# Segment sums, scan and step order in the Mamba mixer of a perceiver block

## The chip, the cores and the metric

The kernel runs on one core of a Trainium2 chip. The metric is device time in microseconds (us), the median of several runs. All arithmetic is float32. A core has five engines with a queue of their own each: TensorE (PE in the profile; its weight loads are PEld), VectorE (DVE), ScalarE (ACT), GpSimd (POOL) and SyncE (SP, which issues the DMAs here). An engine executes its instructions strictly in the order in which they were put down; engines wait for each other by semaphores.

## The reference

A block of three layers with residuals: cross attention of 8 x 64 queries on 8 x 1601 keys (32 heads of 128), a Mamba-2 mixer, and a routed low-rank layer. The change lies in the mixer. Cut to what matters:

```python
proj = einsum('bld,pd->blp', hidden_states, in_proj_w)
gate, hbc, dt = proj[..., :I], proj[..., I:I+CONV_DIM], proj[..., -H:]
conv = conv_bias + sum(pad[:, k:k+L, :] * conv_weight[:, k] for k in range(4))
xBC = silu(conv)                      # x: 64 heads x 64, B and C: 8 groups x 128
dt_p = softplus(dt + dt_bias); dA = exp(dt_p * A); dtx = dt_p * x
state = state * dA_t + dtx_t * B_t    # per head, step by step in time
y_t = einsum('bhpn,bhn->bhp', state, C_t)
y = y + x * D
yn = y * rsqrt(mean(y*y over a group of 512) + eps) * norm_weight * silu(gate)
out = einsum('bli,di->bld', yn, out_proj_w)
```

Here B x L is 8 x 64 tokens of width 512; there are 64 heads in 8 groups.

## The kernel before

**Attention** (the first 2290 us or so) is not touched by the change, and the built program's order there is the same but for line numbers. Then the **mixer** goes through 8 groups of 8 heads; the 512 tokens are four tiles of 128, and each tile holds two sequences (b = 0, 1) of 64 tokens. The recurrence is not run step by step: since a sequence has only 64 tokens, y is a 64 x 64 matrix product per head and sequence, whose matrix is C·B times the decay between two time steps. Per group:

- `steps` (GpSimd, L1154): four `av`, one for each tile, from the decay exponents; four buffers.
- `decay` (TensorE L1170, ScalarE L1175): the segment sums `seg` of two tiles at a time, as 64 x 64 matmuls into two banks of tag `seg`, and their exponentials `dec`. It is called twice, for tiles 0, 1 and for tiles 2, 3. Tag `seg` has two buffers, so the second call's matmuls wait until the first call's two exponentials have read the banks.
- `project` (TensorE L1184): ten input projections of 128 channels by 512 tokens. Numbers 0 to 3 are gates, 4 to 7 are x, 8 and 9 are B and C. For 4 to 9 VectorE makes the convolution's four taps out of the bank (`acc`, L1195 for the first tap and L1201 for the three others), ScalarE the silu (`xs` L1209, `bc` L1207); for x, ScalarE also writes `y` = D·x (L1213), VectorE turns `xs` by 32 x 32 blocks (`xt`, L1216), and SyncE sends it through DRAM (`x_d`) and back as `dx`, which GpSimd multiplies by dt (L1294).
- `project_gates` (TensorE L1246): in groups 1 to 7 the gate projections, as a Strassen-like scheme of seven products in two halves, `first` (four products) and `second` (three more into banks a, b, c). Between them ScalarE copies bank a to `p` (L1261) and VectorE reads d, b and c (`u` L1263, `p` L1264, `sg` L1265); `second` writes into these banks again.
- `mix` (L1284 to L1294): the product C·B of a tile (`pg` on TensorE, in a `seg` bank), masked (`gm`, VectorE) and multiplied by `dec` to `m` (VectorE L1291; two buffers).
- `scan` (TensorE L1307, VectorE L1313): 16 matmuls of 64 x 64 for one tile into the banks y0 and y1 (one buffer each), and two additions to `y`.
- `gate` and `squares`: the squares of y (`sq`, ScalarE L1319), their sums over channels (GpSimd L1320 and L1322, result `s`), and y times the gate (VectorE L1329).
- `norm` (TensorE L1335 `pss`, ScalarE L1338 and L1339 `rs`): the sum over channels and its inverse root.
- `project_out` (TensorE L1348 `mo`, VectorE L1352): a tile of the output projection, added to x. Four tiles a group, in one bank.

ScalarE has two function tables in turn: Silu, and Ln with Exp. Each change is a table load: the one placed ahead of `decay` has L121, the one back is put down with the first silu (L1271 or L1207).

The loop over groups is pipelined by one: while group g is projected, group g - 1 (`old`) is mixed, scanned and gated. Which step of `old` stands behind which projection is written out by hand in the loop (L1435 to L1455); there `issue_after` tells the recording layer to put an instruction down no earlier than another, and within such bounds a planner orders each engine's queue by its own estimate of times. So an engine's order can differ from the text. The last group's own steps stand between its gate projections (L1488 to L1510, `own`).

Of the kernel before, what the change touches and what calls it, by code (L numbers as in the profile page):

```python
# [9 lines left out]
F32 = mybir.dt.float32  # L10
# [5 lines left out]
P = 128  # L16
B, S, D = 8, 64, 512
# [24 lines left out]
H2, PD, N2, G2, KC = 64, 64, 128, 8, 4  # L42
I2 = H2 * PD
HPG = H2 // G2
HH = HPG // 2
GC = I2 // G2 // P
# [72 lines left out]
def load_ln_exp(nc):  # L119

    return nc.scalar.preload_act_table_set("natural_log_exp_and_others")  # L121
# [875 lines left out]
def mixer_and_routed(ctx, tc, c, x, done, w_in, w_out, w_ra, b_w, out):  # L997
# [7 lines left out]
    nc = tc.nc  # L1005

    grpp = ctx.enter_context(tc.tile_pool(name="mx_grp", bufs=2))
# [8 lines left out]
    def bank(tag, shape, name, bufs=1):  # L1016
        return (ps4 if tag in ("pj", "y1") else ps).tile(shape, F32, tag=tag, name=name, bufs=bufs)
# [9 lines left out]
    for g in range(G2):  # L1027
        G = Group()
# [3 lines left out]
    def load_in(G):  # L1032
        g = G.g
        G.w = wst.tile([P, DC, 10, P], F32, tag="w_in", name=f"w_in_{g}")
        at = 0
        for lo, n in (
            (g * GC * P, GC), (I2 + g * GC * P, GC), (2 * I2 + g * N2, 1), (2 * I2 + G2 * N2 + g * N2, 1)
        ):
            nc.sync.dma_start(
                out=G.w[:, :, at : at + n, :],  # L1040
                in_=w_in[:, lo : lo + n * P].rearrange("(dc p) (n o) -> p dc n o", p=P, o=P),
            )
            at += n

    def load_out(G):

        g = G.g
        G.wo = wst.tile([P, GC, D], F32, tag="w_out", name=f"w_out_{g}")
        nc.sync.dma_start(
            out=G.wo, in_=w_out[g * GC * P : (g + 1) * GC * P, :].rearrange("(n p) o -> p n o", p=P)  # L1050
        )
# [18 lines left out]
    for tt in range(NTT):  # L1070
# [5 lines left out]
        for dc in range(DC):  # L1076
            nc.tensor.matmul(
                pdt[:, tt, :], lhsT=xnT[:, dc, tok], rhs=c.wdt[:, dc, :],
                start=dc == 0, stop=dc == DC - 1,
# [49 lines left out]
    for r in range(0, P, S):  # L1129
        nc.tensor.matmul(  # L1130
            psw[r : r + S], lhsT=c.ident[:, S - r : 2 * S - r], rhs=a.rearrange("p t h -> p (t h)"),
            start=True, stop=True,
# [12 lines left out]
    def heads(G):  # L1145
        return slice(G.g * HPG, (G.g + 1) * HPG)

    def steps(G, tt):


        if tt == 0:
            G.av, G.dec = [], grpp.tile([P, NTT, HPG, S], F32, tag="dec", name="dec")
        av = wk.tile([P, 2, HH, S], F32, tag="av", name="av", bufs=4)
        nc.gpsimd.tensor_tensor(  # L1154
            av,
            ah[:, :, tt, G.g, :].unsqueeze(3).to_broadcast([P, 2, HH, S]),
            c.upto1.unsqueeze(1).unsqueeze(1).to_broadcast([P, 2, HH, S]),
            ALU.mult,
        )
        G.av.append(av)  # L1160

    def decay(G, tts):


        segs = [bank("seg", [P, 2, HH, S], f"seg{half}", 2) for half in range(2)]
        for i, tt in enumerate(tts):
            for b in range(2):
                for half in range(2):
                    rows = slice(half * S, (half + 1) * S)
                    nc.tensor.matmul(  # L1170
                        segs[half][b * S : (b + 1) * S, i], lhsT=c.past[rows, rows],
                        rhs=G.av[tt][rows, b], start=True, stop=True,
                    )
        for half in range(2):
            last = nc.scalar.activation(  # L1175
                G.dec[:, tts[0] : tts[0] + 2, half * HH : (half + 1) * HH], segs[half], AF.Exp
            )
        return last.ins
# [100 lines left out]
    def mix(G, tt):  # L1279

        tok = slice(tt * P, (tt + 1) * P)

        pg = bank("seg", [P, P], "pg", 2)
        nc.tensor.matmul(pg, lhsT=G.bc[:, 0, tok], rhs=G.bc[:, 1, tok], start=True, stop=True)  # L1284
        gm = grpp.tile([P, S], F32, tag="gm", name="gm", bufs=2)
        for r in range(0, P, S):
            nc.vector.tensor_tensor(
                gm[r : r + S], pg[r : r + S, r : r + S], c.upto1[r : r + S], ALU.mult
            )
        m = grpp.tile([P, HPG, S], F32, tag="m", name="m")  # L1290
        nc.vector.tensor_tensor(  # L1291
            m, G.dec[:, tt], gm.unsqueeze(1).to_broadcast([P, HPG, S]), ALU.mult
        )
        nc.gpsimd.tensor_tensor(  # L1294
            G.dx[tt], G.dx[tt], dt[:, tt, heads(G)].unsqueeze(2).to_broadcast([P, HPG, PD]), ALU.mult
        )
        G.m = getattr(G, "m", {})
        G.m[tt] = m

    def scan(G, tt):  # L1300

        py = [bank(f"y{b}", [P, GC, S], f"py{b}") for b in range(2)]
        for h in range(HPG):
            r0 = (h % 2) * PD
            for b in range(2):
                at = slice(b * S, (b + 1) * S)
                nc.tensor.matmul(  # L1307
                    py[b][r0 : r0 + PD, h // 2, :], lhsT=G.dx[tt][at, h, :], rhs=G.m[tt][at, h, :],
                    start=True, stop=True,
                )  # L1310
        for b in range(2):
            y = G.y[:, :, tt * P + b * S : tt * P + (b + 1) * S]
            nc.vector.tensor_tensor(y, y, py[b], ALU.add)  # L1313

    def squares(G, tt):
# [50 lines left out]
    def load_routed():  # L1366
        nc.sync.dma_start(out=w, in_=w_ra.rearrange("(dc p) o -> p dc o", p=P))
        nc.sync.dma_start(out=bw, in_=b_w)
# [52 lines left out]
    for tt in (0, 2):  # L1421
        last = decay(g0, (tt, tt + 1))
    for g in range(G2):
        G, old = groups[g], groups[g - 1] if g else None
        new = groups[g + 1] if g + 1 < G2 else None
        load_out(G)
        if new:
            load_in(new)
            for tt in range(NTT):
                steps(new, tt)  # L1430
        elif old:
            load_routed()
        silus = []
        with tc.issue_after(last):


            ns = (8, 9, 4, 5, 6, 7) if new else (4, 5, 6, 7, 8, 9)
            if not old:


                ns = (8, 9, 4, 0, 5, 1, 6, 2, 7, 3)
            for n, behind in zip((None,) + ns, (
                ((mix, 0),),
                ((mix, 1),),
                ((scan, 0),),
                ((mix, 2), (scan, 1)),
                ((gate, 0), (mix, 3), (scan, 2)),
                ((gate, 1), (scan, 3)),
                ((gate, 2), (gate, 3)),
            ) if old else ((),) * (len(ns) + 1)):  # L1450
                if n is not None:
                    done, silu = project(G, n)
                    silus.append(silu)
                if old:
                    with tc.issue_after(done if n is not None else done_out):  # L1455
                        for what, tt in behind:
                            what(old, tt)
            load_x(G)
        if not old:
            token_sums()  # L1460
            sums_in(new, 0)
            sums_in(new, 2)
        with tc.issue_after(silus[-1]):
            table = load_ln_exp(nc).ins
        if new:
            with tc.issue_after(table):
                decay(new, (0, 1))
                last = decay(new, (2, 3))
        if old:
            with tc.issue_after(table):  # L1470
                last = norm(old, range(NTT))

        if not old:
            with tc.issue_after(last):
                weigh_out(G)
            done_out = done
            continue

        def own(*what):

            if not new:
                for step, tt in what:
                    step(G, tt)

        done_out = None
        for k in range(2):  # L1488
            first, second = project_gates(G, 2 * k)
            if k:  # L1490
                own((scan, 3), (squares, 3))
            with tc.issue_after(done_out) if k else nullcontext():
                done_out = first()
            if not k:
                own((mix, 0), (mix, 1))
            with tc.issue_after(done_out):
                done_out = project_out(old, 2 * k)
            if not k:
                own((scan, 0), (squares, 0), (mix, 2))
            with tc.issue_after(done_out), tc.issue_after(last):  # L1500
                done_out, last_gate = second()
            if not k:
                own((scan, 1), (squares, 1), (mix, 3))
            with tc.issue_after(done_out):
                done_out = project_out(old, 2 * k + 1)
            if not k:
                own((scan, 2), (squares, 2))
            if new:
                sums_in(new, 2 * k)
        with tc.issue_after(last_gate):  # L1510
            weigh_out(G)
        last = last_gate

    G = groups[-1]
# [80 lines left out]
```

## Time and profile before

| | |
|---|---|
| median of 3 runs | 2762.47 us (2760.94 to 2763.59) |
| span of the profiled execution | 2760.8 us |
| TensorE busy in it | 2734.8 us (99%) |
| VectorE, ScalarE, GpSimd busy | 63%, 28%, 29% |
| TensorE clock granted | 0.9 or more in every slice |
| start of the first projection of group 0 | 2293.96 us |

Busy time of engines by stage, with the second `mo` tile as the mark between groups 2 to 6 (us of the span):

| stage | length | TensorE | VectorE | ScalarE | GpSimd |
|---|---|---|---|---|---|
| 2293.0 to 2341.0 (group 0) | 48.0 | 47.1 | 30.2 | 18.9 | 12.1 |
| 2341.0 to 2376.0 | 35.0 | 33.8 | 28.9 | 15.6 | 15.0 |
| 2376.0 to 2432.0 | 56.0 | 54.7 | 35.5 | 20.2 | 19.8 |
| 2432.0 to 2487.8 | 55.8 | 54.5 | 35.6 | 19.8 | 19.9 |
| 2487.8 to 2543.7 | 55.9 | 54.6 | 35.6 | 19.9 | 20.0 |
| 2543.7 to 2599.6 | 55.9 | 54.6 | 35.6 | 19.9 | 20.0 |
| 2599.6 to 2654.9 | 55.3 | 54.6 | 35.0 | 19.9 | 15.4 |
| 2654.9 to 2701.4 | 46.5 | 46.4 | 32.4 | 14.2 | 15.1 |
| 2701.4 to 2760.8 (own steps of group 7, routed layer) | 59.4 | 53.5 | 33.6 | 18.9 | 9.7 |

A share of busy time says nothing about who sets the end; that is read from the chain of waits. A line of it has a start, a duration, and an engine with the tile and the line. A line of a timeline has start, busy time, engine, line, operation, output and input tiles, shapes, and in brackets the idle time just before it with what ended it. A matmul in float32 is two records, so x16 are eight matmuls.

### The profile page before, as it was taken

The page shows a single profiled execution, that of the slowest core. Times are in us where ns is not written, and L with a number is a line of the kernel's source. Part 1 is how long each engine was busy: PE and PEld are TensorE (multiplying, and loading weights), DVE is VectorE, ACT ScalarE, POOL GpSimd, SP SyncE. Part 2 cuts the span into 40 slices and gives each one's busy share as a digit, 9 for nine tenths or more (in the row PEclk, how much of TensorE's full clock was granted, in tenths as well). Part 3 has the DMA queues.
Part 4 walks back from the last instruction along what each step waited for, and adds up shares of the span by engine and source line. Part 5 has one row for each costly group of instructions (what it writes and reads, how often), then busy time and mean ns, then how long its engine had stood idle before and what let it go on. Part 6 is the DMA issues. An engine that isn't in the chain of part 4 may idle for free.

```text
span 2760.8 us, 38909 instructions
## 1 busy us (share of the span) xinstructions
PE 2734.8 (99%) x14962; PEld 2003.4 (73%) x14962; DVE 1751.8 (63%) x3151; ACT 772.4 (28%) x1374; POOL 811.5 (29%) x810
## 2 busy tenths in 40 slices
PE   9999999999999999999999999999999999999999
PEld 7677787777777777778777777877777654555555
DVE  5666676576666666766666676667666416765676
ACT  3322223222222222222222222223222103333333
POOL 4423323222222233222322222223322212334321
PEclk9999999999999999999999999999999999999999
DMA  4821322131123212221322132122211462333421
GB/s 164 280 90 47 88 66 61 48 104 43 51 54 89 57 39 85 78 56 40 87 71 55 46 97 55 42 77 66 64 49 52 131 213 66 93 95 100 132 64 35
DMA packets 349715, 222.85 MB, mean 81 GB/s; under 512 B 223932, under 2 KB 309050, under 8 KB 348506
## 3 DMA queue, kind: packets, MB, share of 16 engines
q1 hardware_dynamic: 349530, 220.36, 28.3%
q8 instruction: 119, 1.95, 0.3%
q14 instruction: 66, 0.54, 0.1%
HBM read 189.26 MB, written 31.05 MB: 80 GB/s over the span
## 4 chain that ended last, share of the span: by engine, by line
PE 88%; DVE 8%; DMA 2%; ACT 2%; issue 1%; POOL 1%; SPq 0%; DVEq 0%; ACTq 0%; POOLq 0%
PE pav L623 13%; PE psc L553 13%; PE pv_a L472 6%; PE pv_b L472 6%; PE pk_b L412 6%; PE pv_c L472 6%; PE pk_c L412 6%; PE pk_a L412 6%; PE mo L1348 3%; PE pv_d L472 3%; PE pk_d L412 3%; DVE acc L1201 3%; PE psn L441 2%; PE pj L1184 2%; PE pj_ab L1246 1%; PE pvl L495 1%
## 5 line engine op out<-in xcount | busy, mean ns | idle before, releaser
L558 DVE SCALAR_TENSOR_TENSOR attn<-psc,rk,mask_sb 128x256 f32<-128x256 f32 (+1 forms) x832 | 364.3, 476 | 201.3 <-PE psc L553 199.4
L607 POOL TENSOR_TENSOR sm<-attn 128x512 f32<-128x512 f32 x64 | 81.9, 1280 | 1201.5 <-ACT attn L605 1201.5
L623 PE MATMUL pav<-attn,v 128*128 128x256 f32 (+1 forms) x1664 | 380.3, 379 | 0.0
L553 PE MATMUL psc<-q,kT 128*128 128x256 f32 x1536 | 367.1, 380 | 0.0
L610 POOL TENSOR_TENSOR sm<-sm,attn 128x512 f32<-128x512 f32 x256 | 339.8, 1327 | 29.4 <-DVE attn L601 10.2
L553 PEld LDWEIGHTS psc<-q,kT 128*128 128x128 f32 x1536 | 287.6, 190 | 76.3 <-issue 28.6
L623 PEld LDWEIGHTS pav<-attn,v 128*128 128x128 f32 (+1 forms) x1664 | 311.5, 190 | 42.3 <-issue 1.0
L601 DVE TENSOR_TENSOR attn<-attn,nb 128x1024 f32<-128x1024 f32 x192 | 224.8, 1215 | 48.0 <-ACT nb L598 47.7
L605 ACT ACTIVATE attn<-attn 128x1024 f32<-128x1024 f32 x192 | 203.1, 1058 | 79.8 <-DVE attn L601 77.1
L472 PEld LDWEIGHTS pv_a<-wv,cx 128*128 128x128 f32 x1536 | 193.9, 191 | 28.9 <-issue 22.1
L569 DVE TENSOR_TENSOR mx<-mx,attn 128x512 f32<-128x512 f32 x256 | 211.1, 825 | 2.0
L472 PE MATMUL pv_a<-wv,cx 128*128 128x128 f32 x1536 | 206.8, 277 | 0.0
L412 PE MATMUL pk_a<-cx,wk 128*128 128x417 f32 (+1 forms) x512 | 193.3, 500 | 0.8 <-ACT qrs L115 0.8
L1184 PE MATMUL pj<-mx_xnT,w_in 128*128 128x512 f32 x416 | 190.4, 601 | 0.0
L423 ACT ACTIVATE ksq<-kT 128x834 f32<-128x834 f32 (+1 forms) x128 | 109.2, 871 | 144.7 <-DVE kT L404 144.7
L1184 PEld LDWEIGHTS pj<-mx_xnT,w_in 128*128 128x128 f32 x416 | 74.9, 190 | 78.9 <-issue 75.7
L412 PEld LDWEIGHTS pk_a<-cx,wk 128*128 128x128 f32 x512 | 97.2, 190 | 46.1 <-issue 20.8
L1348 PE MATMUL mo<-w_out,y 128*128 128x512 f32 x256 | 115.8, 594 | 0.0
L598 ACT COPY nb<-nbs 128x256 f32<-128x256 f32 x64 | 24.1, 376 | 301.5 <-DMA nbs<-max_d 289.0
L402 ACT COPY kT<-pk_a 128x384 f32<-128x384 f32 x64 | 31.6, 493 | 267.6 <-PE pk_a L412 267.5
L1201 DVE SCALAR_TENSOR_TENSOR acc<-pj,small_consts,acc 128x504 f32<-128x504 f32 x144 | 104.3, 724 | 1.4
L670 POOL TENSOR_TENSOR o<-o,f 128x512 f32<-128x512 f32 x31 | 39.5, 1274 | 221.4 <-DMA f<-sums_d 184.4
(247 smaller groups left out, 4391.8 us busy)
## 6 DMA issues: line engine op xcount, KB each, us to landing
wk<-in_wk SPq DMA_DIRECT2D x32, 512.0 KB
wv<-in_wv SPq DMA_DIRECT2D x32, 512.0 KB
w_in<-in_w_in SPq DMA_DIRECT2D x16, 1024.0 KB
wvs<-wv_s_d SPq DMA_DIRECT2D x28, 512.0 KB
wks<-wk_s_d SPq DMA_DIRECT2D x28, 512.0 KB
cx<-in_ctxT SPq DMA_DIRECT2D x16, 834.0 KB
cx<-in_ctxT SPq DMA_DIRECT2D x16, 768.0 KB
wq<-in_wq SPq DMA_DIRECT2D x16, 512.0 KB
```

Source lines behind the costliest of these rows:

```text
L412: nc.tensor.matmul(ps[:, :w], lhsT=u.wk[l][:, dc, :], rhs=u.cx.r[ch][r][:, dc, :], start=start and dc == 0, stop=dc == 1, skip_group_check ...
L472: nc.tensor.matmul(ps[:, i * HD : (i + 1) * HD], lhsT=u.cx.r[ch][r][:, dc, i * P : (i + 1) * P], rhs=u.wv[l][:, dc, :], start=start and i ...
L553: nc.tensor.matmul(ps[:rows, t - t2, :], lhsT=lhsT, rhs=qh, start=True, stop=True)
L558: nc.vector.scalar_tensor_tensor(out=s.at[:rows, t, :].rearrange("p (h q) -> p h q", h=GQ), in0=ps[:rows, t - t2, :].rearrange("p (h q) -> ...
L569: nc.vector.tensor_tensor(s.mx2, s.mx2, s.at[:, t2 : t2 + 2, :], ALU.max)
L601: nc.vector.tensor_tensor(at[:, k : k + 4, :], at[:, k : k + 4, :], nb.unsqueeze(1).to_broadcast([P, 4, 256]), ALU.add,)
L605: nc.scalar.activation(at[:, k : k + 4, :], at[:, k : k + 4, :], AF.Exp)
L610: nc.gpsimd.tensor_tensor(sm2, sm2, at[:, i : i + 2, :], ALU.add)
L623: nc.tensor.matmul(s.av[:, 0, :], lhsT=u.v[:rows, t, hh, :], rhs=s.at[:rows, t, :], start=t == 0, stop=t == NKT - 1,)
L1184: done = nc.tensor.matmul(pj, lhsT=G.w[:, dc, n, :], rhs=xnT[:, dc, :], start=dc == 0, stop=dc == DC - 1).ins
L1201: nc.vector.scalar_tensor_tensor(out=accb[:, :, k:], in0=pjb[:, :, : S - k], scalar=c.cw[:, ct, KC - 1 - k : KC - k], in1=accb[:, :, k:], ...
L1348: last = nc.tensor.matmul(po, lhsT=G.y[:, n, tt * P : (tt + 1) * P], rhs=G.wo[:, n, :], start=n == 0, stop=n == GC - 1,)
```

## The change

- `decay` puts the segment sums of tiles 2 and 3 into the banks y0 and y1 of the scan instead of the two `seg` banks, so that the second call's matmuls need not wait for the first call's exponentials.
- `m` has four buffers instead of two.
- `scan` takes two tiles: 32 matmuls into y0 and y1, and two additions of 128 x 512 instead of four of 128 x 256. It is called for pair 0 (tiles 0, 1) and pair 1 (tiles 2, 3).
- The hand-written order of the old group's steps is another: scan of pair 0 stands behind projection 4 (with the third `mix` one projection earlier), gate 0 behind 5, gate 1 and scan of pair 1 behind 6. The last group's own steps are placed anew in the same way.
- The core's scratch for DMAs that GpSimd would issue is 1024 bytes instead of the default.

```diff
     def decay(G, tts):
-        segs = [bank("seg", [P, 2, HH, S], f"seg{half}", 2) for half in range(2)]
+        segs = [
+            bank(f"y{half}", [P, 2, HH, S], f"seg{half}") if tts[0] else
+            bank("seg", [P, 2, HH, S], f"seg{half}", 2) for half in range(2)
+        ]
...
-        m = grpp.tile([P, HPG, S], F32, tag="m", name="m")
+        m = grpp.tile([P, HPG, S], F32, tag="m", name="m", bufs=4)
...
-    def scan(G, tt):
-        py = [bank(f"y{b}", [P, GC, S], f"py{b}") for b in range(2)]
-        for h in range(HPG):
-            r0 = (h % 2) * PD
-            for b in range(2):
-                at = slice(b * S, (b + 1) * S)
-                nc.tensor.matmul(
-                    py[b][r0 : r0 + PD, h // 2, :], lhsT=G.dx[tt][at, h, :], rhs=G.m[tt][at, h, :],
-                    start=True, stop=True,
-                )
+    def scan(G, pair):
+        py = [bank(f"y{b}", [P, 2, GC, S], f"py{b}") for b in range(2)]
+        for i in range(2):
+            tt = 2 * pair + i
+            for h in range(HPG):
+                r0 = (h % 2) * PD
+                for b in range(2):
+                    at = slice(b * S, (b + 1) * S)
+                    nc.tensor.matmul(
+                        py[b][r0 : r0 + PD, i, h // 2, :], lhsT=G.dx[tt][at, h, :], rhs=G.m[tt][at, h, :],
+                        start=True, stop=True,
+                    )
         for b in range(2):
-            y = G.y[:, :, tt * P + b * S : tt * P + (b + 1) * S]
+            y = G.y.rearrange("p n (t b s) -> p b t n s", b=2, s=S)[:, b, 2 * pair : 2 * pair + 2]
             nc.vector.tensor_tensor(y, y, py[b], ALU.add)
...
                 ((mix, 0),),
                 ((mix, 1),),
-                ((scan, 0),),
-                ((mix, 2), (scan, 1)),
-                ((gate, 0), (mix, 3), (scan, 2)),
-                ((gate, 1), (scan, 3)),
+                ((mix, 2),),
+                ((scan, 0), (mix, 3)),
+                ((gate, 0),),
+                ((gate, 1), (scan, 1)),
                 ((gate, 2), (gate, 3)),
...
             if k:
-                own((scan, 3), (squares, 3))
+                own((scan, 1), (squares, 2), (squares, 3))
...
             if not k:
-                own((scan, 0), (squares, 0), (mix, 2))
+                own((mix, 2))
...
             if not k:
-                own((scan, 1), (squares, 1), (mix, 3))
+                own((scan, 0), (squares, 0), (squares, 1), (mix, 3))
...
-            if not k:
-                own((scan, 2), (squares, 2))
...
-    nc = bacc.Bacc("TRN2", target_bir_lowering=False, num_devices=1)
+    nc = bacc.Bacc("TRN2", target_bir_lowering=False, num_devices=1, dynamic_dma_scratch_size=1024)
```

In the built program, the new order of the engines in groups 2 to 6 around these steps is: TensorE has the scan of pair 0 between projections 4 and 5, that of pair 1 between 6 and 7, all 16 segment-sum matmuls of the next group in one burst behind projection 7, then the first half of the gate products, the first two matmuls of the first `mo` tile, the four `pss`, the other two matmuls of that tile, and the second half. ScalarE has, from projection 7 on: `xs`, the table load, `y`, four `dec`, the Ln of `rs`, `p`, the Exp of `rs`, the table load back. Before, `p` stood ahead of that `xs`, and TensorE had the second burst of segment sums behind the first `mo` tile and `pss` within the second half of the gate products. GpSimd now has the first `av` of the next-but-one group between the square sums of tile 3.

## The prediction

> **What bounds the kernel now.** I read the page's chain of waits first, then the chain of one mixer group in order of time, then each engine's timeline in that group. Durations are microseconds; L numbers are lines of the kernel before. The page says TensorE:
>
> ```profile
> PE 88%; DVE 8%; DMA 2%; ACT 2%; issue 1%; POOL 1%; SPq 0%; DVEq 0%; ACTq 0%; POOLq 0%
> ```
>
> That is the whole kernel, and most of it is attention, which the change leaves as it is. The change acts after about 2293 us, in eight groups. The chain through the group that I cost (start, duration, what):
>
> ```profile
> 2448.53 3.45 PE pj L1184 x8
> 2451.98 0.03 issue
> 2452.01 0.81 DVE acc L1195
> ...
> 2478.62 0.72 DVE acc L1201
> 2479.35 0.02 issue
> 2479.37 0.63 ACT xs L1209
> 2480.02 1.28 ACT L121
> 2481.32 0.72 ACT y L1213
> 2482.04 0.49 ACT dec L1175
> 2482.53 0.04 issue
> 2482.57 1.58 PE seg L1170 x16
> ...
> 2487.83 3.43 PE mo L1348 x8
> ```
>
> So in the first half of a group the end is set by VectorE, not by TensorE: from the first convolution of projection 8 (2452.01) to the last one of projection 7 (ends 2479.34) VectorE has no gap to speak of, 27.33 us; then ScalarE does xs, the table load, y and the first dec; only then TensorE goes on. From the mo at 2487.83 to the next group's projection 8 TensorE is back to back. The second burst of segment sums is where TensorE waits (start, busy, idle before in brackets):
>
> ```profile
> 2477.68 3.60 PE L1348 MATMUL mo<-w_out,y 128*128 128x512 f32 x8
> 2482.57 1.58 PE L1170 MATMUL seg<-av,past 64*64 64x256 f32 x16 [1.30 <-ACT dec L1175]
> 2484.08 1.13 PE L1246 MATMUL pj_ab<-mx_xnT,w_in 128*128 128x256 f32 x4
> ```
>
> **What the change removes on TensorE.** The second burst goes into the scan's banks, directly behind the first. From 2481.11 (2477.68 plus 3.43 for the mo) to 2484.08 it cost 2.97; as eight more matmuls of one burst it costs about what the first burst did, 1.02 (2473.10 to 2474.12): 1.95 saved. Four scan bursts become two. A scan burst issues for 0.63 (2455.55 to 2456.18), and the projection behind it takes 3.54 instead of the undisturbed 3.43, the one before it 3.52: 0.2 a burst, 0.4 a group. [...]
>
> If TensorE set the end here, a group would lose 2.35. It doesn't, so I follow the chain.
>
> **What takes the wait's place.** In the built program's new order ScalarE has, in groups 1 to 6: xs, table, y, four dec in a row, the Ln of rs (L1338), and only then p (L1261), which before stood ahead of xs. The second half of the gate products may not overwrite bank a until p has read it. So the wait that went from the segment sums comes back at the products, behind four dec and not one. Rows of ScalarE:
>
> ```profile
> 2477.01 0.37 ACT L1261 COPY p<-pj_ab 128x256 f32<-128x256 f32 x1 [1.31 <-PE pj_ab L1246]
> ...
> 2481.94 1.06 ACT L1175 ACTIVATE dec<-seg 128x512 f32<-128x512 f32 x2
> 2484.19 1.08 ACT L1175 ACTIVATE dec<-seg 128x512 f32<-128x512 f32 x2 [1.18 <-PE seg L1170]
> 2486.03 0.26 ACT L1338 ACTIVATE rs<-pss,eps 128x4 f32<-128x4 f32 x1 [0.76 <-PE pss L1335]
> ```
>
> Counted from the start of the first dec: dec starts follow each other by 0.48 (1.06 less one dec's 0.58), so the Ln starts at 1.92, p at 2.10, p ends at 2.47; TensorE is released 0.04 later (as at 2482.53), at 2.51. Three products of 0.86 follow, plus 0.1 to 0.2 after a stop, and bank c also waits until VectorE has done u, p, the x update (which now stands between them) and sg (0.44 + 0.34 + 0.67 + 0.42 after p: 4.36, against 4.25 to 4.4 from TensorE). So the second mo starts 5.2 to 5.35 after the first dec. Before it was 2487.67 - 2481.94 = 5.73. This tail gives 0.45. TensorE itself would be ready for the products at about 2482.7, p ends at about 2483.8: 1.1 of the saved time goes into the new wait. Behind p on ScalarE stand the Exp of rs, the table load and the gates' silu; the second half's mo waits for none of them longer than this.
>
> **The VectorE stretch.** Same work, other order; I add up start-to-start steps taken from the rows at 2452 to 2479. A step is 0.72 for a first tap (0.84 if its second tap comes directly behind), 0.65 and 0.63 for the others between other work, 0.76 directly behind each other, gm 0.13 and 0.26, m 0.60, xt 0.63, gate 0.60. The merged add (128x512) is in no row: at least twice the shorter part of a 128x256 add (0.33 step, 0.41 long), so 0.60 to 0.66; I take m's step, 0.60, as its nearest row (0.68 long, same width). New order: projections 8 and 9 with gm and m of tiles 1 and 2: 2 x 3.76, to 2459.53. Projection 4 and two adds: 0.84 + 0.76 + 0.65 + 0.60 + 0.63 + 0.60, to 2463.61. gm, xt (waits 0.04 for xs), gm, m: to 2465.27. Projections 5 and 6 with gates 0, 1, xt and the second pair's adds: 8.3, to 2473.57. Projection 7 with gates 2, 3 and xt: 0.71 + 0.60 + 0.63 + 0.64 + 0.60 + 0.76 + 0.72, to 2478.2. That is 1.1 less than 2479.34, half of it from fewer adds and less waiting, half from this:
>
> ```profile
> 2476.23 1.02 DVE L1329 TENSOR_TENSOR y<-y,sg 128x512 f32<-128x512 f32 x1
> 2477.82 0.88 DVE L1329 TENSOR_TENSOR y<-y,sg 128x512 f32<-128x512 f32 x1
> ```
>
> A gate otherwise takes 0.69 (2459.40), and in group 6, where no av runs on GpSimd, 0.68 at both places. Here GpSimd's two av run from 2475.66 to 2478.15: 0.33 + 0.19, some 0.55 of the stretch. In the new order av come free at once after the burst (about 2474.9), and GpSimd has the square sum of tile 3 and an av beside gate 3 (2476.2), and that of tile 2 beside gate 2 (2474.3). I take 0.55 again; bounds 0 and 1.1. [...]
>
> Stretch shorter by 0.55, tail by 0.45: **1.0 a group in groups 2 to 5**, 4.0.
>
> **The other groups.** Group 6 has no av before either, so only waiting and adds are saved, 0.35 + 0.45: 0.8. Group 1: TensorE now stops at pg, whose bank the first dec frees (2335.82 plus about 0.35, since one more projection matmul of 0.86 comes after the first merged burst, whose second half waits for the av anyway), and projection 8 is done at about 2339.9 as before; its stretch, added the same way, ends at 2367.5 to 2368 against 2367.80, and the x update ahead of p on VectorE eats the tail: 0. Group 7 has no dec. There both tiles' squares now come after one pair's adds: adds end about 2697.7, two squares (0.63), two sums on GpSimd of 1.0 and 0.9 each (2699.07 to 2701.02 for one tile now), so the last pss is at 2701.6 to 2702.3, not 2701.08, and mo follows: 0.9 to 1.5 lost; its own four scans as two bursts give back 0.4. Net 0.8 lost. m with four buffers lets m of tiles 1 and 2 be made before the first scan; the stretch has the same count of them, so nothing. The smaller DMA scratch: no row of the trace shows a transfer from GpSimd's queue (q1 is the only data queue), so 0.
>
> Sum: 4.0 + 0.8 + 0 - 0.8 = 4.0 off the profiled execution: span 2760.8, 1.7 below the median of 2762.47. So 2756.8 for its span, 2758.5 for the median; I say **2758**. A measurement of this kernel can tell about 0.2% from no change, 5.5 us: below 2756.9 is faster, above 2768.0 slower. Bounds: merged add 0.60 to 0.66 (0.25 a group), GpSimd 0 to 1.1 (0.55 either way), tail 0.35 to 0.55: 1.0 is 0.2 to 1.65 a group, times five, group 1 and 7 +-0.7: 2754 to 2763 for this case.
>
> **Rivals.** (1) TensorE is the bound and what it saves comes off: 2.35 x 6 = 14, 2748. For it: the page's 99% busy and 88% of the chain. Against: the chain above, 30.5 of a group's 55.9 us (2452.0 to 2482.5) through VectorE and ScalarE, and p behind the dec. Something of it would show if p's wait were hidden: 1.1 a group more, 2752. Chance 0.17 for 2754 or less.
> (2) Nothing left: av slow both gates fully, adds slow, 2761 to 2767. For it: order puts av between the sums. 0.18.
> (3) Slower: two squares now stand together on ScalarE ahead of xs, and four VectorE instructions per group (gate 0, xt, gate 2, xt) are queued right behind them with as little as 0.03 to spare. Each that waits for one square costs 0.63; all four are 2.5 a group, 1.5 net, times five, plus 0.8: 2770. It decides from about 2 us of such waits a group. Against: my times have each of them just ready. 0.08.
> (4) The burst isn't one: its second half must wait for the second pair's adds. They end at about 2473.0, the half is due at 2473.9; and if late, up to 5 us are covered by the stretch. It changes no time, and is within the forecast.
> Forecast 0.57. Of it some 0.25 lie below 2756.9. Faster: 0.17 + 0.25 = 0.42; slower 0.08 and 0.02 from (2): 0.10; within: 0.48. Range 2752 to 2764, leaving about one in ten on each side.
>
> **What would show it.** Right: one burst of 32 seg records a group, no wait there; a wait of about 1 us at pj_ab's second products, released by p; last tap of projection 7 at 26.6 to 27 us after the first; groups 55.87 apart now 54.9; group 7 a little longer. Wrong: if TensorE has no wait at p, (1); if VectorE's stretch is 27.3 or more with waits for ScalarE's squares, (3) or (2).

## The result, and the profile after

The changed kernel is slower: 2781.33 us median of 4 runs (2778.49 to 2785.69), against 2762.19 (2760.94 to 2763.59) for the kernel before on the same chip. The ratio is 1.0071, 95% interval 1.0057 to 1.0086; I had said 2758. The profiled execution has a span of 2776.7 us, 15.9 more than before. Attention ended 2.2 us earlier in it; in the profiles of all the kernels here, which share it, its end varies from 2291.8 to 2296.5. The mixer's groups 0 and 1 lost 5.2 together, group 2 3.3, groups 3 to 5 2.15 each, group 6 2.25, group 7 1.6, and what follows gained 0.7. Of the kernels below, busy3, segs_only and segs_back_busy2 had one execution each that was disturbed and took two to four times as long; the ratios leave it out, it shifts a median by 0.3 us at most, and in segs_back_busy2 it is the profiled one, so that there is no profile to compare.

I take the same group as in the prediction (line numbers from `scan` on are a few higher now). The chain of waits of the changed kernel, in order of time (start, duration, what):

```profile
2458.31 0.81 DVE acc L1198
...
2485.11 0.74 DVE acc L1204
2485.87 0.63 ACT xs L1212
2486.52 1.28 ACT L121
2487.82 0.72 ACT y L1216
2488.54 0.49 ACT dec L1178
2489.03 0.14 issue
2489.16 1.02 PE pss L1340 x8
2490.19 3.16 PE mo L1353 x4
...
2496.30 3.43 PE mo L1353 x8
```

Up to the first dec the chain is the old one: VectorE from 2458.31 to 2485.85 (27.54 us; 27.33 before), then ScalarE. The burst of segment sums that waited for this dec is gone from the chain, and `pss` stands in its place. From the start of the first dec (2488.44) to the second mo (2496.13) it is 7.69 us; before it was 5.73. TensorE's timeline of the changed kernel there:

```profile
2478.62 2.32 PE L1173 MATMUL seg<-av,past 64*64 64x256 f32 x32
...
2484.43 1.88 PE L1353 MATMUL mo<-w_out,y 128*128 128x512 f32 x4
2489.16 1.02 PE L1340 MATMUL pss<-ones,s 128*128 128x1 f32 x8 [2.86 <-ACT dec L1178]
2490.05 3.30 PE L1353 MATMUL mo<-w_out,y 128*128 128x512 f32 x4
2493.15 1.42 PE L1249 MATMUL pj_ab<-mx_xnT,w_in 128*128 128x256 f32 x4
```

The one burst is there (32 records), and no wait in it. But `pss` is a tile of tag `seg`, whose two banks hold the sums of tiles 0 and 1 until the first dec has read one of them. It stands after two of the first mo tile's matmuls, so TensorE stops for 2.86 us in the middle of that tile, and everything behind stops with it. All six groups with a next group do this: `pss` waits 16.0 us for `dec` in all.

The second thing to see is the length of the two mo matmuls behind the stop: 3.30 us, where the tile's other two, ahead of it, took 1.88. The windows of the same stretch (start and end, length, busy time with counts of PE, PEld, DVE, ACT and POOL, then the granted TensorE clock, DMA share and GB/s):

```profile
2484.43:2486.30 1.87, 1.87 (x5) 0.57 (x3) 1.37 (x3) 0.43 (x1) 1.87 (x3) 1.00 0.45 71
2486.30:2489.10 2.80, 0.01 (x1) 0.00 (x0) 0.71 (x1) 2.77 (x5) 1.45 (x2) 1.00 0.28 44
2489.10:2490.00 0.90, 0.84 (x8) 0.87 (x8) 0.00 (x0) 0.90 (x3) 0.00 (x0) 1.00 0.75 117
2490.00:2493.10 3.10, 3.10 (x6) 1.32 (x6) 0.84 (x2) 2.28 (x5) 0.00 (x0) 0.59 0.37 103
2493.10:2494.40 1.30, 1.30 (x5) 1.05 (x4) 0.94 (x2) 0.00 (x0) 0.00 (x0) 0.68 1.00 293
```

After the stop the granted clock falls. The 0.59 and 0.68 are means of windows that lie partly in the drop; cut at its edges, it is half the clock, from 2490.53 to 2493.94:

```profile
2489.90:2490.50 0.60, 0.60 (x4) 0.42 (x4) 0.00 (x0) 0.60 (x4) 0.00 (x0) 1.00 0.51 81
2490.55:2493.90 3.35, 3.35 (x6) 1.66 (x5) 1.28 (x3) 1.73 (x4) 0.00 (x0) 0.50 0.48 164
2493.95:2496.10 2.15, 2.15 (x11) 1.89 (x10) 0.59 (x2) 0.38 (x1) 0.58 (x1) 1.00 0.81 225
```

By the rows it costs 1.44 us on the two mo matmuls (3.16 in the chain, less 2 x 0.86) and 0.40 on the two products behind (2493.15 to 2494.41, 1.26 and not 0.86): 1.84 of the group's 2.15. That is a little too much, since two mo matmuls directly behind `pss` take 1.80 and not 1.72 from start to start at the full clock too (busy3 below). TensorE has no gap in the drop, so 3.41 us at half the clock should cost half of that, 1.71. The kernel before stopped for 1.30 us at its second burst in this group and kept 1.00 in every group; its window around that stop:

```profile
2480.99:2484.40 3.41, 2.11 (x19) 0.99 (x18) 0.06 (x1) 2.22 (x5) 0.58 (x1) 1.00 0.50 77
```

### The profile page after: what moved, and what is told of

Read it like the earlier page. It is cut to its first block, busy times and chain, and to the rows that moved or that the text cites. A ratio compares the mean times of both kernels' runs of the same rounds, so it can differ in the third digit from the quotient of the medians.

```text
span 2776.7 us, 38861 instructions
## 1 busy us (share of the span) xinstructions
PE 2737.3 (99%) x14962; PEld 2006.6 (72%) x14962; DVE 1752.9 (63%) x3119; ACT 768.4 (28%) x1374; POOL 812.3 (29%) x810
## 4 chain that ended last, share of the span: by engine, by line
PE 88%; DVE 8%; DMA 2%; ACT 1%; POOL 1%; issue 1%; SPq 0%; DVEq 0%; ACTq 0%; POOLq 0%
PE pav L623 13%; PE psc L553 12%; PE pv_a L472 6%; PE pv_b L472 6%; PE pk_b L412 6%; PE pv_c L472 6%; PE pk_c L412 6%; PE pk_a L412 6%; PE mo L1353 4%; PE pv_d L472 3%; PE pk_d L412 3%; DVE acc L1204 3%; PE pj L1187 2%; PE psn L441 2%; PE pj_ab L1249 1%; PE pvl L495 1%
## 5 line engine op out<-in xcount | busy, mean ns | idle before, releaser
L1353 PE MATMUL mo<-w_out,y 128*128 128x512 f32 x256 | 124.6, 627 | 0.0
```

What stands on the lines that cost most here:

```text
L1353: last = nc.tensor.matmul(po, lhsT=G.y[:, n, tt * P : (tt + 1) * P], rhs=G.wo[:, n, :], start=n == 0, stop=n == GC - 1,)
```

## The experiments

Two theories stood at the start. One: the place of `pss` in a `seg` bank makes the stop, and the stop lowers the clock. The other: the paired scan and the new order cost by themselves, by VectorE and GpSimd colliding. The period below is the distance of two second mo tiles, in groups 2 to 5 of each kernel's profiled execution; the stops are TensorE's in such a group. Each ratio is taken against runs of the kernel before on the same chip, whose medians lay between 2762.2 and 2763.1.

| kernel | median, us | ratio to before, 95% | period, us | stops on TensorE, us | clock falls |
|---|---|---|---|---|---|
| before | 2762.2 | | 55.87 | 1.30 | no |
| changed | 2781.33 | 1.0071 (1.0057 to 1.0086) | 58.02 | 2.86 | yes |
| segs_back | 2779.5 | 1.0061 (1.0046 to 1.0076) | 57.7 to 60.7 | 2.27 | yes |
| segs_only | 2776.65 | 1.0045 (1.0031 to 1.0058) | 57.84 | 2.25 | yes |
| busy0 | 2777.67 | 1.0054 (1.0039 to 1.0069) | 58.02 | 2.86 | yes |
| busy3 | 2768.6 | 1.0022 (1.0012 to 1.0031) | 56.35 | 0.28 | no |
| segs_back_busy2 | 2763.62 | 1.0001 (0.9992 to 1.0011) | | | no |
| mo_then_pss | 2776.41 | 1.0047 (1.0030 to 1.0063) | 58.04 | 1.14 and 1.61 | yes |
| p_first | 2755.46 | 0.9973 (0.9961 to 0.9984) | 54.60 | 0.94 and 0.48 | no |
| p_first_seg | 2774.47 | 1.0038 (1.0023 to 1.0053) | 57.76 | 0.94 and 1.75 | yes |
| before_p_first | 2756.94 | 0.9977 (0.9967 to 0.9988) | 54.60 | 0.31 | no |
| p_first_av8 | 2755.7 | 0.9976 (0.9966 to 0.9985) | 54.60 | 0.95 and 0.48 | no |
| p_first_mo | 2752.66 | 0.9962 (0.9949 to 0.9976) | 54.07 | 0.94 | no |
| scratch | 2762.6 | 1.0002 (0.9992 to 1.0011) | 55.88 | 1.30 | no |

The row of segs_back_busy2 has times alone; its clock is the mean that its runs were granted, 0.999 to 1.000.

**segs_back** undoes the bank change alone, on the changed kernel:

```diff
-        segs = [
-            bank(f"y{half}", [P, 2, HH, S], f"seg{half}") if tts[0] else
-            bank("seg", [P, 2, HH, S], f"seg{half}", 2) for half in range(2)
-        ]
+        segs = [bank("seg", [P, 2, HH, S], f"seg{half}", 2) for half in range(2)]
```

> The changed kernel with one edit undone: the segment sums of tiles 2 and 3 go into the seg banks again, as a second burst. The paired scan, the step order, the buffers of m and the scratch stay. Theory (the norm sums pss and all behind them on TensorE wait for the first dec because the seg banks are held, and the clock falls after that stop): with pss free early there is no stop of over 2 us in front of it, the granted clock is 1.00 in every group, and group 3 goes from C0 to the second mo tile in about 36.1 us (35.9 of the kernel before plus the 0.21 by which VectorE's stretch grew); time 2760 to 2767. Rival (the paired scan and the step order are what costs, by contention of VectorE and GpSimd): time stays at 2775 or above.

Measured: 2779.5. My first theory missed here. `pss` no longer waits for the dec, and the loss stays. TensorE's timeline of segs_back, and its windows:

```profile
2484.01 3.60 PE L1350 MATMUL mo<-w_out,y 128*128 128x512 f32 x8
2489.88 2.20 PE L1170 MATMUL seg<-av,past 64*64 64x256 f32 x16 [2.27 <-ACT dec L1175]
2492.01 2.08 PE L1246 MATMUL pj_ab<-mx_xnT,w_in 128*128 128x256 f32 x4
```

```profile
2489.80:2492.00 2.20, 2.12 (x16) 0.84 (x16) 0.00 (x0) 0.51 (x2) 0.69 (x1) 0.70 0.45 70
2492.00:2494.00 2.00, 2.00 (x9) 1.63 (x6) 0.00 (x0) 1.08 (x2) 1.36 (x2) 0.50 0.40 137
```

It is the kernel before in its order: first mo tile, second burst, products. But the first mo starts 24.9 us after the first tap of projection 8 (2459.12) and not 25.7: TensorE has no gap of note up to there in either kernel, and with two scan bursts instead of four, in the new order, its work is 0.8 shorter (the prediction had 0.4). The dec comes no earlier (30.1 us after that tap, 29.9 in the kernel before). So TensorE arrives 0.8 us sooner and waits 2.27 us at the same place instead of 1.30, and the clock falls (0.70 and 0.50 as means of these windows). That gave the theory its second form: whatever shortens TensorE's work ahead of this wait lengthens the stop, and a stop of these 2.27 us costs clock where the 1.30 of the kernel before did not.

**segs_only** is the kernel before with the bank change alone (the diff above, the other way round).

> The kernel before with one edit of the change alone: the segment sums of tiles 2 and 3 go into the y banks, in one burst. Theory: pss stands in the first mo tile and waits about 2.5 to 3 us for the first dec, the clock falls below 0.7 behind it, and the time is 2772 to 2782, nearly the whole loss. Rival (paired scan and step order cost): 2757 to 2764, the second burst's 1.95 us per group won or hidden.

Measured: 2776.65, with a stop of 2.25 at `pss` and half the clock behind it:

```profile
2490.60 1.02 PE L1338 MATMUL pss<-ones,s 128*128 128x1 f32 x8 [2.25 <-ACT dec L1178]
```

```profile
2492.55:2495.90 3.35, 3.35 (x8) 1.91 (x7) 1.74 (x4) 1.19 (x1) 0.00 (x0) 0.50 0.67 217
```

Each of the two parts alone makes three quarters or more of the loss (17 and 14 of 19 us), and both together are not twice as bad. That fits a cost that is paid once per stop, not the rival, by which this kernel would have been no slower.

**busy0 and busy3** ask whether the wait or the clock costs. Both are the changed kernel with `pss` held where it stood; the loop of the diff is in busy3 alone, and adds TensorE work:

```diff
         po = bank(tag, [P, D], "mo", 3 if tag == "pj" else 1)
+        for _ in range(3 if between else 0):
+            nc.tensor.matmul(
+                po, lhsT=G.y[:, 0, tt * P : (tt + 1) * P], rhs=G.wo[:, 0, :], start=True, stop=True
+            )
...
+            if between and n == 1:
+                between(last.ins)
```

> The changed kernel with pss pinned by hand behind the second matmul of the first mo tile, which is where it stood: a control for the next kernel. All theories: as the changed kernel, 2776 to 2785, with the stop of over 2 us ahead of pss and a clock below 0.7 behind it.

> As the control, with three more matmuls of 128x128 by 512 in groups 1 to 7, which stand ahead of the first mo tile's own and are overwritten by them: they do part of the product again, and TensorE has some 2.6 us more to do in each group, in the time in which it waits for the first dec. If the lowered clock behind the stop is what costs (1.8 of the 2.15 us per group): the remaining stop is under 1 us, the clock stays at 1.00, and the kernel with more work is faster than the control by 7 to 12 us, 2766 to 2773. If the wait alone costs: equal to the control within 2 us, or slower by up to 18 (seven times 2.6) where the work doesn't fit into the wait.

Measured: 2777.67 and 2768.6: with 2.58 us more matmul work per group (an estimate, 3 x 0.86) the kernel is 9.1 us faster than busy0. TensorE's timeline of busy3 (L1353 are the added matmuls, L1357 the tile's own), and its window behind the stop:

```profile
2481.09 2.74 PE L1353 MATMUL mo<-w_out,y 128*128 128x512 f32 x6
2483.66 1.88 PE L1357 MATMUL mo<-w_out,y 128*128 128x512 f32 x4
2485.82 1.02 PE L1340 MATMUL pss<-ones,s 128*128 128x1 f32 x8 [0.28 <-ACT dec L1178]
2486.70 1.96 PE L1357 MATMUL mo<-w_out,y 128*128 128x512 f32 x4
```

```profile
2485.80:2488.50 2.70, 2.68 (x12) 1.64 (x13) 1.00 (x3) 2.65 (x7) 0.00 (x0) 1.00 0.32 50
```

`pss` still starts when the dec allows it; only the stop is filled, and the two mo matmuls behind it take 1.96 us again instead of 3.30. The period is 56.35 against 58.02: 1.67 us a group is the clock, close to the 1.71 of a drop of 3.41 us. The other 0.48 above the kernel before is 0.20 in the stretch up to the dec and 0.28 behind it, since `pss` and half a mo tile now follow the dec.

**segs_back_busy2** puts two such matmuls into segs_back in the same way, and holds the second burst behind the first mo tile, where it stood.

> The kernel with the segment sums of tiles 2, 3 put back into the seg banks (2779.5 us, stop of 2.27 us ahead of their burst, clock 0.67 and 0.50 behind it), with two more matmuls of 128x128 by 512 ahead of the first mo tile's own, which overwrite them: part of the product is done twice, 1.72 us more for TensorE in groups 1 to 7. Theory (a stop of about 2 us lowers the clock, and that is what costs, whichever part of the change makes the stop): the stop shrinks to about 0.6 us, the clock stays 1.00, and the time is 2762 to 2767, 12 to 17 us faster than without the added work. Rival (paired scan and step order cost by themselves): 2775 or above.

Measured: 2763.62, 16 us less than segs_back. So the loss of the other half of the change goes with its stop too. That it is the clock is read from the mean granted clock (0.999 to 1.000, where segs_back has 0.992 to 0.996); the stop itself was not seen.

**mo_then_pss** moves `pss` behind the whole first mo tile (in the diff of busy0, `n == 3` for `n == 1`).

> The changed kernel with pss behind all four matmuls of the first mo tile instead of behind two; all else as changed. Theory: the wait for the first dec is filled with the other two mo matmuls, the stop is 2.86 - 1.72 = about 1.1 us, the clock stays 1.00, and the second mo tile starts 35.7 to 36.0 us after C0 less 1.7: the time is 2755 to 2764. Rival (the dec chain and p behind it set the second products, not the place of pss): 2772 or above.

Measured: 2776.41, a miss. TensorE's timeline, and the window behind it:

```profile
2481.79 3.60 PE L1353 MATMUL mo<-w_out,y 128*128 128x512 f32 x8
2486.52 1.02 PE L1340 MATMUL pss<-ones,s 128*128 128x1 f32 x8 [1.14 <-ACT dec L1178]
2489.16 1.10 PE L1249 MATMUL pj_ab<-mx_xnT,w_in 128*128 128x256 f32 x4 [1.61 <-DVE p L1267]
2490.09 1.86 PE L1249 MATMUL pj_ab<-mx_xnT,ws 128*128 128x256 f32 x4
```

```profile
2490.10:2493.40 3.30, 3.30 (x9) 2.64 (x8) 0.03 (x1) 0.38 (x1) 1.37 (x3) 0.51 0.75 273
```

The stop at `pss` shrank to 1.14 as expected, but the two matmuls that fill it are missing later: the products now wait 1.61 us for `p`, which stands behind four dec on ScalarE. This is the wait that the prediction had named; in the changed kernel it lay under the slowed mo. Behind the two stops, with only the narrow `pss` between them, the clock was 0.51, as it was 0.50 behind the one stop of 2.86 us in the changed kernel. The rival's range was met: with `pss` out of the way, the dec chain and `p` set the second products.

**p_first and p_first_seg** take both waits away: the first gate products and the copy to `p` go ahead of the table load, the decay and the norm; `pss` goes into a `pj` bank (p_first) or stays in `seg` (p_first_seg). The core of p_first:

```diff
-        pss = bank("seg", [P, NTT], "pss", 2)
+        pss = bank("pj", [P, NTT], "pss", 3)
...
-        with tc.issue_after(silus[-1]):
+        begun = None
+        if old:
+            first, second, st = project_gates(G, 0)
+            begun = first(), second, st.copied
+        with tc.issue_after(silus[-1]), tc.issue_after(begun[2]) if begun else nullcontext():
             table = load_ln_exp(nc).ins
```

> The changed kernel with the first gate products and the copy of p put down ahead of the table load, the decay and the norm, and pss in a pj bank, so that neither pss nor the second products stand behind dec. Theory: no wait for dec is left on TensorE before the second mo tile, only that for the first x update (rs behind the four dec); the second mo tile comes about 33.5 to 34 us after C0 (35.9 in the kernel before), stops stay under 1.5 us and the clock at 1.00: 2745 to 2752. Rival (TensorE's earlier arrival only makes a longer stop, at rs): a stop of over 1.8 us with a lowered clock behind it, 2760 to 2775.

> As the one before, but pss in a seg bank as in the changed kernel. Theory: pss stands ahead of all of the first mo tile and waits for the first dec, a stop of over 3 us with a lowered clock behind it: 2775 to 2795. Rival (the bank of pss doesn't matter): within 3 us of the one before.

Measured: 2755.46 and 2774.47. The bank of `pss`, with the place that it then gets in TensorE's order, is worth 19 us here. Both ranges were missed slightly: the planner put two mo matmuls ahead of `pss` in p_first_seg, so its stop was 1.75 and not over 3, with half the clock behind it (0.51 from 2488.30 to 2491.70 in group 3); and p_first keeps two stops. TensorE's timeline of p_first:

```profile
2471.82 1.13 PE L1249 MATMUL pj_cd<-mx_xs,ws 128*128 128x256 f32 x4 [0.94 <-DVE acc L1204]
...
2477.05 1.02 PE L1340 MATMUL pss<-ones,s 128*128 128x1 f32 x8 [0.48 <-DVE acc L1204]
2477.93 3.68 PE L1353 MATMUL mo<-w_out,y 128*128 128x512 f32 x8
```

In the middle groups nothing on TensorE waits for a dec or for `p` any more ahead of the second mo tile; what is left is VectorE's last tap, which holds the `pj` banks.

**before_p_first** is the same rearrangement on the kernel before, without the change.

> The kernel before, with only what the fastest kernel so far (2755.46 us, ratio 0.9973) has beside the change: the first gate products and the copy of p ahead of the table load, the decay and the norm, and pss in a pj bank; two bursts of segment sums, the scan by one tile and the old order. It tells what the change itself is worth where no stop follows from it. Theory (the change saves TensorE some 1.95 + 0.4 us per group, which count once neither pss nor p waits for dec): this kernel is slower than 2755.5, since the second burst still waits for the first dec in the middle of the second products: 2759 to 2768. Rival (the gain is the reordering alone): 2753 to 2757.

Measured: 2756.94, where p_first has 2755.46 (their intervals overlap), and the same period, 54.60. The rival holds: the gain is the rearrangement. In this order the change's shorter work on TensorE shows as a longer stop, 0.94 + 0.48 against 0.31, and buys nothing although the clock stays up (a mean of 1.000 and 0.999 in the profiled executions).

**p_first_av8** gives `av` eight buffers.

> The fastest kernel so far with eight buffers of av instead of four, so that GpSimd's last four av products (4.04 us) run early and not beside VectorE's third and fourth gate. Theory (the fourth gate takes 0.90 to 1.38 us beside GpSimd and 0.68 to 0.8 without, and VectorE's stretch sets when TensorE may go on): VectorE's stretch is shorter by 0.1 to 0.5 us per group, 2751 to 2755. Rival (the av products only collide with other VectorE work, earlier): 2754 to 2758.

Measured: 2755.7, period 54.60: the theory missed. The edit didn't do what it was for: four `av` still start right behind the burst of segment sums in every such group, as in p_first. So what the collision with GpSimd is worth was not measured by an edit.

**scratch** has the smaller DMA scratch alone.

> The kernel before with only the smaller scratch for DMA descriptors. All theories: no change, 2760 to 2765, stages as before. If it were slower by over 3 us, part of the loss would not be in the mixer's groups.

Measured: 2762.6 against 2762.7. It does nothing.

**p_first_mo** is p_first with `pss` behind the first mo tile, so that the 0.48 is filled.

> The fastest kernel so far (2755.46 us) with pss behind all of the first mo tile instead of ahead of it, so that the 0.48 us for which pss waits for the last tap's pj bank are filled by mo. Theory: the period of a middle group falls from 54.60 to about 54.1 us, since the second products and the second mo tile follow without a stop, and the time to 2751 to 2754, the clock staying at 1.00. Rival (the x update, whose rs now comes later and behind the four dec, or p takes the stop over): period 54.4 to 54.7, 2754 to 2757.

Measured: 2752.66, the fastest kernel of the study, period 54.07 as worked out. That is 0.53 a group less than before_p_first, where `pss` waits for nothing that its move could fill, so some of the change's shorter work on TensorE seems to come off here. It was not tried on the kernel before, and the two ratios' intervals overlap. TensorE's timeline:

```profile
2472.47 1.96 PE L1173 MATMUL seg<-av,past 64*64 64x256 f32 x32
2474.36 3.70 PE L1353 MATMUL mo<-w_out,y 128*128 128x512 f32 x8
2477.89 0.95 PE L1340 MATMUL pss<-ones,s 128*128 128x1 f32 x8
2478.70 1.11 PE L1249 MATMUL pj_ab<-mx_xnT,w_in 128*128 128x256 f32 x4
```

## Why the prediction was wrong

- **What bounds the group** was right: VectorE's stretch and ScalarE's chain to the first dec. Rival 1 (TensorE is the bound, 2748) is out: the group grew by 2.15, and before_p_first and p_first have the same period, so that in their order too the saved work doesn't reach the end.
- **TensorE's saving** happened about as stated: one burst, no wait in it, of 2.25 us (2478.62 to 2480.87) where the sum had 2.04; in segs_back the work up to the first mo tile was 0.8 shorter where the sum had 0.4 for the scans. That it doesn't come off was stated too; that it could make the kernel slower was not.
- **The step that failed** is "TensorE itself would be ready for the products at about 2482.7". It let `pss` run ahead of the products as soon as its inputs were there. The code says that `pss` takes a `seg` bank, and the built order showed it in the middle of the first mo tile; put together, they place a wait for the first dec ahead of the second half of the tile and the products. I followed what the second burst had waited for, and not who else waits for the same banks. The wait that took its place was therefore `pss`, not `p`; measured from the dec, the tail is 7.69 and not 5.2 to 5.35.
- **The clock was in no term of the sum.** The profile before showed 1.00 with a stop of 1.30, and I took every wait for its length alone. Of the tail's excess over 5.73, 1.96, the clock makes 1.67 by busy0 and busy3 (up to 1.84 by the rows); the other 0.29 is `pss` and half a mo tile, which now follow the dec.
- **p behind four dec** was sized well. ScalarE's timeline of the changed kernel:

```profile
2488.44 2.04 ACT L1178 ACTIVATE dec<-seg 128x512 f32<-128x512 f32 x4
2490.35 0.28 ACT L1343 ACTIVATE rs<-pss,eps 128x4 f32<-128x4 f32 x1
2490.49 0.40 ACT L1264 COPY p<-pj_ab 128x256 f32<-128x256 f32 x1
```

  It starts 2.05 us after the first dec (2.10 predicted) and ends at 2.45 (2.47). It decides in mo_then_pss and in group 1, where TensorE stops for it 1.33 us more, with the x update ahead of `p` on VectorE, as the prediction had it there. Group 1 was put at 0 and made most of the 5.2: besides these 1.33 us TensorE stops for 2.17 at `pss`, and the clock is at half from 2371.06 to 2377.89.
- **VectorE's stretch** was to fall to 26.75 and rose to 27.54. The merged add was right (0.67 long, a step of 0.60). Of the 0.79 by which the stretch came out longer, 0.26 is the piece with gm, xt, gm and m behind projection 4 (1.92, not 1.66) and 0.50 the collision with GpSimd, which was mis-sized. VectorE's timeline of the changed kernel, gates 2 and 3:

```profile
2481.07 0.81 DVE L1334 TENSOR_TENSOR y<-y,sg 128x512 f32<-128x512 f32 x1
...
2483.06 1.38 DVE L1334 TENSOR_TENSOR y<-y,sg 128x512 f32<-128x512 f32 x1
```

  With 0.68 as the undisturbed length these two lose 0.13 and 0.70, and gate 0 (0.90) 0.22: 1.05, not the 0.55 that I took, and near the upper bound of 1.1. GpSimd runs from 2482.17 to 2484.74 without a gap beside the long one (a square sum, an `av`, a sum); the `av` ends at 2483.88, and the gate at 2484.44. Why this gate lost 0.70, where I had extrapolated 0.33 and 0.19 from the kernel before, was not shown.
- **Rival 3** gave the right sign for a reason that didn't come about: the four instructions it names (gates 0 and 2, at 2472.57 and 2481.07, and the xt behind them) follow what stands before them without a wait. **Group 7** lost 1.6 us where I had 0.8; `pss` waits there for the sums on GpSimd, as stated, 1.61 and 0.29. The sum's lower bound of 0.2 a group comes out at 0.1 from its own terms (1.0 less 0.25, 0.55 and 0.1), which moves the range by half a microsecond.

## What to carry to other kernels

When an edit takes a wait away, list every tile that shares the freed or held banks, and find its place in the in-order queue: the next one of that tag is the next wait. Less work on an engine that waits anyway made its stop longer here (2.27 us in segs_back, 1.30 in the kernel before). On TensorE each of the changed kernel's six stops of 2.17 to 2.86 us at `pss` cost the clock as well, some 1.7 us (1.67 by busy0 and busy3) on top of its length for a drop of 3.41 us, so such a stop is better filled with work that is due anyway than left longer. What helps is to move the awaited thing (here the copy to `p`, and `pss` out of the held bank) ahead of the chain that is late.

## What the runs showed of the hardware

The granted clock fell after short stops of TensorE, and to half: in windows of 0.5 us through the mixer of the changed kernel it is 1.00 or 0.50, and a figure between them is the mean of a window that lies partly in a drop. Each of its six stops of 2.17 to 2.86 us at `pss` brought a drop, and so did the stops of 2.27 us (segs_back) and 2.25 (segs_only) shown above. The kernel before kept 1.00 through its stops of 1.09 to 1.31 us, and p_first had a mean of 1.000 with stops of 0.94 and 0.48 five microseconds apart. In between both happened: behind 1.75 us in p_first_seg, where a stop of 0.94 had ended 8.4 us earlier, the clock was 0.51, and behind 1.80 in group 1 of p_first it was 1.00. In mo_then_pss it was 0.51 behind two stops, 1.14 and 1.61, with only `pss` between them. The two stops at `pss` in group 7 of the changed kernel, 1.61 and 0.29, brought no drop.

In those windows the drops of the changed kernel come out as 6.83 us long in groups 1 and 2 and as 3.41 in groups 3 to 6. By the means of the windows at their edges they start at 2371.06, 2429.09, 2490.53, 2548.55, 2606.58 and 2664.61: 58.02 or 58.03 us apart, but 61.44 from group 2 to group 3. The stops end at 2369.33, 2429.87, 2489.16, 2547.18, 2605.20 and 2662.76. So a drop started between 0.78 us ahead of the end of its stop and 1.85 us behind it, and two stops of nearly the same length, 2.85 in group 2 and 2.86 in group 3, came with drops of 6.83 and 3.41.

In the 3.41 us ahead of the drop of group 3 TensorE was busy for 1.37 us; in the window of the kernel before that is shown above, as long and around its stop, for 2.11, with the clock at 1.00. What sets the start and the length of a drop, and which stops bring one, was not tried by itself and stays open.
